# Maxima of the unkept key tiles: score tiles compared with keys on the partitions, in place of products with queries on the partitions

## The chip, the cores and the metric

One core of a Trainium2 chip runs the whole kernel. The metric is the device time of one execution in microseconds; the time shown for a kernel is the median of its runs. One further execution is recorded by the hardware profiler, and the profile's views (busy shares, groups of instructions, timeline, windows, the chain of waits) all tell of that one.

The engines are named as in the profile: PE is TensorE (matrix products; PEld is its weight load), DVE is VectorE, ACT is ScalarE, POOL is GpSimd, and SP issues most of the DMAs. Products go to PSUM[...].

## The reference

Input `x` is (2, 2048, 512) float32, and `cond_1024` is a conditioning vector for each of the two batches. Two blocks follow each other.

1. A conditioned state-space block: a modulated layer norm, a diagonal complex linear recurrence along the 2048 positions (128 states), a gated residual, and then a modulated feed-forward with 2048 hidden features (gelu).
2. A conditioned attention block with 16 heads of 32 features:

```python
h = _sln(hidden, w, ...)                    # layer norm, scaled and shifted by the condition
q, k, v = split(h @ Wqkv.T + bqkv)          # 16 heads of 32
energy = einsum('bhqd,bhkd->bhqk', q, k)
att = softmax(energy, axis=-1) / D ** 0.5
out = einsum('bhqk,bhkd->bhqd', att, v)     # back to (B, N, 512)
out = out @ Wp.T + bp
h1 = out + hidden
return _sln(h1, w, ...) + h1
```

The softmax needs, for each query, the maximum of its scores over all 2048 keys before the exponentials. The change concerns how this maximum is found for a part of the keys.

## The kernel before

**Two parts.** The first part (to about 1400 us) does the state-space block, the feed-forward and the projections to q, k and v, in chunks of 512 positions. Queries, keys and values are written to DRAM, q and k as a high and a low half each (`hi`, `lo`), so that one product with 128 rows of contraction gives the scores of 32 features at close to float32 precision. The second part is the attention, and the change lies in it.

**Blocks and slots.** The attention runs over 64 blocks: a batch, a pair of heads and a chunk of 512 queries. Keys stand in 16 tiles of 128. A score tile `s` is 128 keys on the partitions by 512 queries for each of the two heads, so 128 x 1024 float32, or two PSUM banks. A block is spread over NP = 8 slots (index `i`), and two blocks are under way at a time: in slot `j` the kernel finds maxima for the block that begins 14 slots later (AHEAD), and does exponentials and weighted sums for the block that is current. The code writes the work of each slot in the order in which every engine shall take it (the schedule is manual), and semaphores between engines come from what each instruction reads and writes. A tile of a pool with `bufs=n` takes its turn in a ring of n buffers; a new tile waits until the one that held its buffer before has been read.

**The maxima.** Of the 16 key tiles, NX = 11 are kept: `keep` (L761) makes the score tile on PE (`raw_scores`, L751), ACT copies it to SBUF (L765), and DVE takes the running maximum of the block over it (L770, `runs[n]`). Slots i = 0, 2 and 6 keep two tiles, the others one. The other five tiles (NY) are not kept; their scores are made again later by `make` (L815) in five slots (i = 1, 3, 4, 5, 7), when DVE subtracts the maximum straight from PSUM. For the maxima of these five, `across` (L772) computes in each of the eight slots the scores of 128 queries of one head against all 640 keys, with queries on the partitions (two products of 320 columns into the two banks of tile `m`), and DVE reduces them along the row (L784).

`turn_run` (L786) transposes the running maximum of a block on PE, so that queries stand on the partitions, and DVE reduces over keys (L791); a last reduction (L794) joins this with the results of `across`. These run in slots i = 1 and 2 of the next block, and `spread` (L798) in i = 3: it writes the negated maximum to DRAM and reads it back on all partitions as `shift`.

**The rest of a slot.** `take_off` (L811) adds `shift` to a kept tile on POOL, `exponentials` (L822) runs on ACT, and `weighted` (L827) sums values weighted by the probabilities on PE into `o`, for the two key tiles of the slot before. The order in a slot is: what is due by the table `due`; `make`; `across`; a first exponential; `keep`; a second exponential; work due later in the slot; `take_off`; `weighted`. When a block is finished ACT copies `o` out (L843).

**Output.** Batch 0's output projection, residual and norm run in slots of batch 1's blocks (`project`, `residual`, `statistics`, `gain`), with the projection in the PSUM tag `pt`. For the last batch `project` takes its PSUM tile from the tag `m` (L901), and for the last chunk `end_begin` (L1036) takes one from `m` and one from `s`.

**PSUM in the attention:** `s` two tiles of two banks, `m` two banks, `pt` one and `o` one: eight.

Of the kernel before, what the change touches and what calls it, by code (L numbers as in the profile page):

```python
# [8 lines left out]
F32 = mybir.dt.float32  # L9
# [5 lines left out]
ALU = mybir.AluOpType  # L15
AX = mybir.AxisListType
# [3 lines left out]
P = 128  # L20
# [19 lines left out]
def tile_s5_block_then_sln_attention(  # L40
# [21 lines left out]
    nc = tc.nc  # L62
    NB, L, D = x.shape
    KC = D // P
    CH = 512
    TT = CH // P
# [4 lines left out]
    NKT = L // P  # L71
# [4 lines left out]
    small = ctx.enter_context(tc.tile_pool(name="small", bufs=2))  # L76
# [436 lines left out]
    def at_norm(b, c):  # L513
        normalised(b, c)
        xc = xt.pop((b, c))
        for t in range(TT):
            nc.gpsimd.tensor_tensor(xc[:, t, :], xc[:, t, :], bp_row, ALU.add)
        nc.sync.dma_start(x2[b][c * CH : (c + 1) * CH, :].rearrange("(t p) d -> p t d", p=P), xc)
# [40 lines left out]
    start = order[0]  # L559
# [68 lines left out]
    for i, now in enumerate(order):  # L628
# [36 lines left out]
        def run_due(at):  # L665
            for what, *args in due[at]:
                what(*args)
# [27 lines left out]

    NX = 11
    NY = NKT - NX  # L700
    YW = NY * P // 2
    kpools = [ctx.enter_context(tc.tile_pool(name="kpool0", bufs=2, side="right"))]
    qpool = ctx.enter_context(tc.tile_pool(name="qpool", bufs=4, side="right"))
    ring = ctx.enter_context(tc.tile_pool(name="ring", bufs=22, side="right"))
# [1 line left out]
    ps = ctx.enter_context(tc.tile_pool(name="ps2", bufs=1, space=PSUM, side="right"))  # L706
# [15 lines left out]
    pair_of = [pairs.index((b, p)) for b, p, _ in blocks]  # L722
    kst, qst, shifts, runs, tops = {}, {}, {}, {}, {}
    kept, probs, outs, ends = {}, {}, {}, {"o": [], "by": []}
# [24 lines left out]
            nc.sync.dma_start(vst[i % 2][:, :, 2 * e, :], vd[b][:, f].rearrange("(t p) d -> p t d", p=P))  # L749

    def raw_scores(n, kt):  # L751
        s = ps.tile([P, 2, CH], F32, name="s", bufs=2)
        for e in range(2):
            nc.tensor.matmul(  # L754
                s[:, e, :], kst[pair_of[n], e][:, kt * P : (kt + 1) * P], qst[n][:, e, :],
                start=True, stop=True,
            )
        return s


    def keep(n, kt):  # L761

        s = raw_scores(n, kt)
        x = ring.tile([P, 2, CH], F32, name="x")
        nc.scalar.copy(x, s)  # L765
        kept[n, kt] = x
        if kt == 1:
            runs[n] = rows_r.tile([P, 2, CH], F32, name="run")
        if kt > 0:
            nc.vector.tensor_tensor(runs[n], s, kept[n, 0] if kt == 1 else runs[n], ALU.max)  # L770

    def across(n, e, t):  # L772

        if (e, t) == (0, 0):
            tops[n] = small.tile([P, 2 * TT, 2], F32, name="top", bufs=3)
        m = ps.tile([P, 2, CH], F32, name="m")
        for i in range(2):
            k = NX * P + i * YW
            nc.tensor.matmul(  # L779
                m[:, i, :YW], qst[n][:, e, t * P : (t + 1) * P], kst[pair_of[n], e][:, k : k + YW],  # L780
                start=True, stop=True,
            )
        j = e * TT + t
        nc.vector.tensor_reduce(tops[n][:, j, 0:1], m[:, :, :YW], AX.XY, ALU.max, negate=True)  # L784

    def turn_run(n, e):  # L786

        pt = ps.tile([P, TT, P], F32, name="pt_run", tag="pt")
        for t in range(TT):
            nc.tensor.transpose(pt[:, t, :], runs[n][:, e, t * P : (t + 1) * P], ident)  # L790
        nc.vector.tensor_reduce(tops[n][:, e * TT : (e + 1) * TT, 1], pt, AX.X, ALU.max, negate=True)  # L791
        if e == 1:
            neg = small.tile([P, 2 * TT], F32, name="neg", bufs=3)
            nc.vector.tensor_reduce(neg, tops[n], AX.X, ALU.min)  # L794
            tops[n] = neg
            runs.pop(n)

    def spread(n):  # L798
# [12 lines left out]
    def take_off(n, kt):  # L811
        x = kept[n, kt]
        nc.gpsimd.tensor_tensor(x, x, shifts[n], ALU.add)  # L813

    def make(n, kt):  # L815

        s = raw_scores(n, kt)
        x = ppool.tile([P, 2, CH], F32, name="pT")
        nc.vector.tensor_tensor(x, s, shifts[n], ALU.add)  # L819
        kept[n, kt] = x  # L820

    def exponentials(n, kt):  # L822
        x = kept.pop((n, kt))
        nc.scalar.activation(x, x, AF.Exp)  # L824
        probs[n, kt] = x
# [69 lines left out]
    def project(b, qt, groups=tuple(range(NG))):  # L895

        o4, h, *py = held[b, qt]
        if py:
            py = py[0]
        elif len(groups) == NG:  # L900
            py = ps.tile([P, 2, CH], F32, name="py2", tag="m")[:, 0, :]  # L901
        else:
            py = ps.tile([P, CH], F32, name="py", tag="pt")
        for g in groups:
            nc.tensor.matmul(py, o4[:, g, :], wp[:, g, :], start=g == 0, stop=g == NG - 1)  # L905
        held[b, qt] = o4, h, py
# [128 lines left out]

    def end_begin(i):  # L1036

        if i:
            ends["py", i] = ps.tile([P, 2, CH], F32, name="py4", tag="s", bufs=2)
        else:  # L1040
            ends["py", i] = ps.tile([P, 2, CH], F32, name="py3", tag="m")
        for t in range(2):
            nc.tensor.matmul(ends["py", i][:, t, :], ident, ends["h"][i][:, t, :], start=True, stop=False)

# [9 lines left out]
    def end_last(o):  # L1054
# [4 lines left out]
        for at in parts:  # L1059
            nc.scalar.copy(raw[:, at], o[:, at])  # L1060
        end_begin(1)
        for i, at in enumerate(parts):
            nc.tensor.matmul(turned[:, i, :], ends["turn"], raw[:, at], start=True, stop=True)
# [49 lines left out]
    keeps, m = [], 0  # L1113
# [5 lines left out]
    for i in range(NP):  # L1119
        if (i + AHEAD) % NP in twice:  # L1120
            uses.append([kx, kx + 1])
            kx += 2
        else:
            uses.append([kx, ky])
            kx += 1
            ky += 1
    assert m == NX and kx == NX and ky == NKT

    due = {}
# [21 lines left out]
    for b in range(NB):  # L1151
        for c in range(NQ):
            j = NP * (blocks.index((b, NPAIR - 1, c)) + 1) + 1
            if (b, c) == (LB, LC):
                most, rest = slice(0, NH - 4), slice(NH - 4, NH - 2)
                j = NP * (N - 1)
# [22 lines left out]
            for t in range(TT):  # L1179
                qt = c * TT + t  # L1180
                if b == LB:
                    k = j + 3 + 2 * t
# [8 lines left out]
                else:  # L1191

                    k = NP * (NPAIR * NQ * (b + 1) + 2 + 3 * qt // 2)
# [15 lines left out]
    def block_at(j):  # L1209
        n, i = divmod(j, NP)  # L1210
        return (n, i) if 0 <= n < N else (None, i)

    for j in range(FIRST, NP * N + 2):
        if j == OPEN:
            assert not left
            late.close()
            fixed = ctx.enter_context(tc.tile_pool(name="fixed", bufs=1))
            kpools.append(ctx.enter_context(tc.tile_pool(name="kpool1", bufs=2)))
            ppool = ctx.enter_context(tc.tile_pool(name="ppool", bufs=2))
            rows = ctx.enter_context(tc.tile_pool(name="rows", bufs=2))  # L1220
            work = ctx.enter_context(tc.tile_pool(name="work2", bufs=2))
            ps_o = ctx.enter_context(tc.tile_pool(name="ps_o", bufs=1, space=PSUM))
            vst = [fixed.tile([P, NKT, 3, HD], F32, name=f"v{i}") for i in range(2)]
            for v in vst:
                nc.gpsimd.memset(v[:, :, 1, :], 1.0)
            wp = fixed.tile([P, KC, D], F32, name="wp")
        if j == 2 * NP + 6:
            nc.sync.dma_start(wp, w_pT.rearrange("(k p) f -> p k f", p=P))
        if j == 4 * NP:
            nc.gpsimd.tensor_scalar(wp, wp, ISQ, None, ALU.mult)  # L1230
        run_due(j)
        n, i = block_at(j + AHEAD)
        todo = list(keeps[i]) if n is not None else []
        now, k = block_at(j)
        if now is not None and uses[k][1] >= NX:
            make(now, uses[k][1])
        if n is not None:
            across(n, i // TT, i % TT)
        if now is not None:
            exponentials(now, uses[k][0])  # L1240
        for kt in todo:
            keep(n, kt)
        if j == -AHEAD - 1:
            pieces = TT
        elif -AHEAD <= j < -AHEAD + 2:
            pieces = 2
        elif j >= -AHEAD + 2:
            pieces = -(-len(left) // (OPEN - j)) if j < OPEN else 0
        else:
            pieces = 0  # L1250
        for _ in range(pieces):
            what, *args = left.pop(0)
            what(*args)
        if j == -AHEAD - 1:
            at_norm(*order[-1])
        if now is not None:
            exponentials(now, uses[k][1])
        run_due(j + 0.5)
        n, i = block_at(j + 1)
        if n is not None:  # L1260
            for kt in uses[i]:
                if kt < NX:
                    take_off(n, kt)
        n, i = block_at(j - 1)
        if n is not None:
            for h, kt in enumerate(uses[i]):
                weighted(n, kt, i == 0 and h == 0, i == NP - 1 and h == 1)
# [56 lines left out]
```

## Time and profile before

| | us |
|---|---|
| median of 3 runs (3457.08 to 3461.29) | 3458.43 |
| the profiled execution | 3459.56 |
| its span, first to last instruction | 3457.8 |
| PE busy in the span | 3335.5 (96%) |
| DVE, ACT, POOL busy | 2151.7, 1939.8, 2137.8 |
| DVE maxima over kept tiles, L770 | 640 of 1.22 each |
| DVE reductions of `m`, L784 | 512 of 0.815 each |
| PE products of scores, L754, and of `m`, L779 | 2048 and 1024 |

A row of the timeline gives start, length, engine, line and operation, out<-in with the shape, and how many instructions were merged; in brackets stands the idle time before it and what ended it. PE's products are pipelined and their ends are modelled, so the distance from one start to the next says more than a row's length. A row of the chain of waits gives start, length and work; the chain leads from the last instruction back to what released each step. A window's row gives its length, then the busy time of PE, PE's weight loads, DVE, ACT and POOL with the number of instructions, then TensorE's granted clock, the DMA share and GB/s.

### The profile page before, as it was taken

Reading aid. Unit: us, or ns where it says so; the run is one execution under the profiler, and the core shown is the slowest. Engines: PE = TensorE matmul, PEld = TensorE weight load, DVE = VectorE, ACT = ScalarE, POOL = GpSimd, SP = SyncE. Lnnn points to the kernel's source line nnn. Section 1 sums busy time; section 2 is a strip of 40 time slices with the busy share of each in tenths; the row PEclk is TensorE's granted clock in tenths of the full one; section 3 lists DMA queues with packets and bytes.
Section 4 is the critical chain, followed back from the end, with each engine's and each line's share of the span. In section 5 each row is a group of like instructions: output and inputs, shape, how many; then the busy total and the mean of one; then the engine's idle time right before and its main releaser. Section 6 shows DMA issues by size and latency. Waiting matters only on the chain.

```text
span 3457.8 us, 34348 instructions
## 1 busy us (share of the span) xinstructions
PE 3335.5 (96%) x11764; PEld 1508.3 (44%) x11764; DVE 2151.7 (62%) x2976; ACT 1939.8 (56%) x2208; POOL 2137.8 (62%) x1162
## 2 busy tenths in 40 slices
PE   7999999999999999999999999999999999999997
PEld 4444444444444444444444444444444444444432
DVE  6232323232322310688888888888888888888885
ACT  2111111111111111398999999999888888888963
POOL 4133131313131310289898989998898989899986
PEclk8999999999999999999999999999999999999999
DMA  8001111111110112432223222223234233233233
GB/s 304 1 31 43 43 43 43 43 43 43 43 43 31 43 37 61 121 77 67 58 62 72 66 67 54 72 67 75 70 81 96 65 87 85 71 85 78 61 97 115
DMA packets 201396, 237.06 MB, mean 69 GB/s; under 512 B 89544, under 2 KB 118728, under 8 KB 197126
## 3 DMA queue, kind: packets, MB, share of 16 engines
q1 hardware_dynamic: 201222, 234.87, 24.5%
q8 instruction: 93, 1.52, 0.2%
q14 instruction: 81, 0.66, 0.1%
HBM read 166.77 MB, written 67.76 MB: 68 GB/s over the span
## 4 chain that ended last, share of the span: by engine, by line
PE 73%; DVE 14%; ACT 8%; issue 2%; DMA 1%; POOL 1%; SPq 0%; DVEq 0%; ACTq 0%; POOLq 0%
PE o L834 15%; PE ph L487 13%; PE po L500 13%; PE s L754 10%; DVE run L770 10%; PE pk L530 6%; ACT x L765 4%; PE pv L542 3%; PE m L779 3%; PE py L905 2%; PE pt_run L790 2%; ACT pT L824 2%; ACT x L824 2%; PE pu L421 2%; PE pt_tf L149 1%
## 5 line engine op out<-in xcount | busy, mean ns | idle before, releaser
L813 POOL TENSOR_TENSOR x<-x,shift 128x1024 f32<-128x1024 f32 x704 | 1653.8, 2387 | 153.6 <-DMA shift<-flat 104.6
L765 ACT COPY x<-s 128x1024 f32<-128x1024 f32 x704 | 692.4, 1012 | 213.0 <-PE s L754 211.9
L770 DVE TENSOR_TENSOR run<-s,run 128x1024 f32<-128x1024 f32 x576 | 702.9, 1220 | 73.6 <-ACT x L765 50.2
L824 ACT ACTIVATE x<-x 128x1024 f32<-128x1024 f32 x704 | 739.8, 1060 | 11.9 <-POOL x L813 11.6
L754 PE MATMUL s<-qs,ks 128*128 128x512 f32 x2048 | 669.5, 421 | 51.3 <-DVE run L770 45.2
L834 PE MATMUL o<-x,v 128*64 128x512 f32 x2816 | 718.4, 612 | 0.0
L487 PE MATMUL ph<-fT,w_sb 128*128 128x512 f32 x1024 | 463.5, 597 | 0.0
L500 PE MATMUL po<-w_sb,hid 128*128 128x512 f32 x1024 | 460.3, 592 | 0.0
L754 PEld LDWEIGHTS s<-qs,ks 128*128 128x128 f32 x2048 | 334.4, 189 | 275.4 <-DVE run L770 149.7
L819 DVE TENSOR_TENSOR pT<-s,shift 128x1024 f32<-128x1024 f32 x320 | 389.5, 1217 | 85.1 <-PE s L754 85.1
L784 DVE TENSOR_REDUCE top<-m 128x1 f32<-128x640 f32 x512 | 417.4, 815 | 9.8 <-PE m L779 7.1
L491 ACT ACTIVATE hid<-ph,vec 128x512 f32<-128x512 f32 x128 | 88.0, 687 | 595.9 <-PE ph L487 595.9
L824 ACT ACTIVATE pT<-pT 128x1024 f32<-128x1024 f32 x320 | 339.4, 1061 | 50.2 <-DVE pT L819 50.2
L158 DVE SCALAR_TENSOR_TENSOR lo<-pk,vec,hi 128x512 fp32r<-128x512 f32 x64 | 48.0, 751 | 494.4 <-ACT hi L157 494.4
L834 PE MATMUL o<-pT,v 128*64 128x512 f32 x1280 | 330.5, 595 | 7.9 <-ACT pT L824 7.9
L487 PEld LDWEIGHTS ph<-fT,w_sb 128*128 128x128 f32 x1024 | 193.3, 192 | 228.9 <-issue 228.9
L834 PEld LDWEIGHTS o<-x,v 128*64 128x64 f32 x2816 | 157.1, 135 | 310.4 <-issue 191.4
L434 POOL TENSOR_TENSOR m<-m,m 128x512 f32<-128x512 f32 x8 | 13.1, 1643 | 449.7 <-DVE m L432 449.7
L500 PEld LDWEIGHTS po<-w_sb,hid 128*128 128x128 f32 x1024 | 190.7, 190 | 221.5 <-issue 221.5
L779 PE MATMUL m<-ks,qs 128*128 128x320 f32 x1024 | 256.6, 332 | 17.3 <-DVE top L784 15.5
L157 ACT ACTIVATE hi<-pk,vec 128x512 fp32r<-128x512 f32 x64 | 44.0, 687 | 383.3 <-PE pk L530 383.3
L510 POOL TENSOR_TENSOR x<-x,gated 128x512 f32<-128x512 f32 x32 | 39.6, 1269 | 354.4 <-DVE gated L509 354.4
(253 smaller groups left out, 2774.6 us busy)
## 6 DMA issues: line engine op xcount, KB each, us to landing
ks<-kd SPq DMA_DIRECT2D x128, 256.0 KB
qs<-qd SPq DMA_DIRECT2D x512, 64.0 KB
shift<-flat SPq DMA_DIRECT2D x64, 512.0 KB
x<-in_x SPq DMA_DIRECT2D x8, 1024.0 KB
w_sb<-in_w SPq DMA_DIRECT2D x8, 1024.0 KB
x<-x SPq DMA_DIRECT2D x8, 1024.0 KB
kd<-hi SPq DMA_DIRECT2D x32, 256.0 KB
kd<-lo SPq DMA_DIRECT2D x32, 256.0 KB
```

The lines of the kernel that those rows point to most:

```text
L487: nc.tensor.matmul(ph, w1_sb[:, k, f * P : (f + 1) * P], fts[b, c][:, k, :], start=k == 0, stop=k == KC - 1)
L500: nc.tensor.matmul(pos[b, c][:, t, :], hid[:, t * P : (t + 1) * P], w2_sb[:, f, :], start=f == 0, stop=f == FC - 1,)
L530: nc.tensor.matmul(pk, w[:, k, g * P : (g + 1) * P], hT[:, k, :], start=k == 0, stop=k == KC - 1)
L754: nc.tensor.matmul(s[:, e, :], kst[pair_of[n], e][:, kt * P : (kt + 1) * P], qst[n][:, e, :], start=True, stop=True,)
L765: nc.scalar.copy(x, s)
L770: nc.vector.tensor_tensor(runs[n], s, kept[n, 0] if kt == 1 else runs[n], ALU.max)
L779: nc.tensor.matmul(m[:, i, :YW], qst[n][:, e, t * P : (t + 1) * P], kst[pair_of[n], e][:, k : k + YW], start=True, stop=True,)
L784: nc.vector.tensor_reduce(tops[n][:, j, 0:1], m[:, :, :YW], AX.XY, ALU.max, negate=True)
L813: nc.gpsimd.tensor_tensor(x, x, shifts[n], ALU.add)
L819: nc.vector.tensor_tensor(x, s, shifts[n], ALU.add)
L824: nc.scalar.activation(x, x, AF.Exp)
L834: nc.tensor.matmul(outs[n][64 * e : 64 * e + 64, :], v[:, kt, e : e + 2, :], x[:, e, :], start=first, stop=final,)
```

## The change

`across` and its PSUM tile `m` are gone. In their place `compare` makes one score tile of an unkept key tile, in the same form as `raw_scores` gives for the kept ones (keys on the partitions), and DVE takes it into the running maximum `runs[n]`. It is called at the place of `across`, in the five slots i = 1, 2, 4, 6 and 7, for key tiles 11 to 15. Nothing is copied to SBUF. The two banks that `m` had go to a third score tile: `s` now has three buffers. `turn_run` alone gives the negated maximum, so the reduction that joined two results goes. `project` (last batch) and `end_begin` take their tiles from the tag `s`.

```diff
     def raw_scores(n, kt):
-        s = ps.tile([P, 2, CH], F32, name="s", bufs=2)
+        s = ps.tile([P, 2, CH], F32, name="s", bufs=3)
...
-    def across(n, e, t):
-
-        if (e, t) == (0, 0):
-            tops[n] = small.tile([P, 2 * TT, 2], F32, name="top", bufs=3)
-        m = ps.tile([P, 2, CH], F32, name="m")
-        for i in range(2):
-            k = NX * P + i * YW
-            nc.tensor.matmul(
-                m[:, i, :YW], qst[n][:, e, t * P : (t + 1) * P], kst[pair_of[n], e][:, k : k + YW],
-                start=True, stop=True,
-            )
-        j = e * TT + t
-        nc.vector.tensor_reduce(tops[n][:, j, 0:1], m[:, :, :YW], AX.XY, ALU.max, negate=True)
+    def compare(n, kt):
+
+        nc.vector.tensor_tensor(runs[n], raw_scores(n, kt), runs[n], ALU.max)
 
     def turn_run(n, e):
 
+        if e == 0:
+            tops[n] = small.tile([P, 2 * TT], F32, name="neg", bufs=3)
         pt = ps.tile([P, TT, P], F32, name="pt_run", tag="pt")
         for t in range(TT):
             nc.tensor.transpose(pt[:, t, :], runs[n][:, e, t * P : (t + 1) * P], ident)
-        nc.vector.tensor_reduce(tops[n][:, e * TT : (e + 1) * TT, 1], pt, AX.X, ALU.max, negate=True)
+        nc.vector.tensor_reduce(tops[n][:, e * TT : (e + 1) * TT], pt, AX.X, ALU.max, negate=True)
         if e == 1:
-            neg = small.tile([P, 2 * TT], F32, name="neg", bufs=3)
-            nc.vector.tensor_reduce(neg, tops[n], AX.X, ALU.min)
-            tops[n] = neg
             runs.pop(n)
...
-            py = ps.tile([P, 2, CH], F32, name="py2", tag="m")[:, 0, :]
+            py = ps.tile([P, 2, CH], F32, name="py2", tag="s", bufs=3)[:, 0, :]
...
-        if i:
-            ends["py", i] = ps.tile([P, 2, CH], F32, name="py4", tag="s", bufs=2)
-        else:
-            ends["py", i] = ps.tile([P, 2, CH], F32, name="py3", tag="m")
+        ends["py", i] = ps.tile([P, 2, CH], F32, name="py4", tag="s", bufs=3)
...
+    compares = dict(zip((1, 2, 4, 6, 7), range(NX, NKT)))
...
-        if n is not None:
-            across(n, i // TT, i % TT)
+        if n is not None and i in compares:
+            compare(n, compares[i])
```

More of the change, by code (lines that the diff above doesn't have):

```diff
@@ L699, in tile_s5_block_then_sln_attention @@
     NX = 11
-    NY = NKT - NX
-    YW = NY * P // 2
     kpools = [ctx.enter_context(tc.tile_pool(name="kpool0", bufs=2, side="right"))]
```

## The prediction

> **What bounds the kernel now.** First the busy shares on the page, then one window of the attention part, then the rows of one slot, then the chain of waits. The page and a window of 200 us in the first half of the attention:
>
> ```profile
> PE 3335.5 (96%) x11764; PEld 1508.3 (44%) x11764; DVE 2151.7 (62%) x2976; ACT 1939.8 (56%) x2208; POOL 2137.8 (62%) x1162
> 1800.00:2000.00 200.00, 195.27 (x850) 87.60 (x851) 176.73 (x183) 185.60 (x204) 181.73 (x79) 1.00 0.26 66
> ```
>
> In the window (PE, weight loads, DVE, ACT, POOL) TensorE is busy 97.6%, but ACT 93%, POOL 91% and DVE 88%: nothing has room for much. The copies of `o` (L843) start 28.50 us apart there, block after block, so that is a block's price; in the second half, where the output projection of batch 0 runs beside, three blocks in turn take 33.05, 29.62 and 31.95 (31.5 on average).
>
> TensorE's timeline over two slots, i=6 and i=7 of a block (start, length, operation):
>
> ```profile
> 1816.19 0.56 PE L779 MATMUL m<-ks,qs 128*128 128x320 f32 x2
> 1816.60 1.09 PE L754 MATMUL s<-qs,ks 128*128 128x512 f32 x4
> 1817.61 1.08 PE L834 MATMUL o<-x,v 128*64 128x512 f32 x4
> 1818.52 1.03 PE L834 MATMUL o<-pT,v 128*64 128x512 f32 x4
> 1819.62 0.73 PE L754 MATMUL s<-qs,ks 128*128 128x512 f32 x2
> 1820.18 0.45 PE L779 MATMUL m<-ks,qs 128*128 128x320 f32 x2
> 1820.95 0.73 PE L754 MATMUL s<-qs,ks 128*128 128x512 f32 x2 [0.31 <-DVE run L770]
> 1821.61 1.94 PE L834 MATMUL o<-x,v 128*64 128x512 f32 x8
> 1823.48 0.56 PE L779 MATMUL m<-ks,qs 128*128 128x320 f32 x2
> ```
>
> Start to start, slot i=6 is m 0.41, two score pairs 1.01, eight `o` 1.87: 3.29 us. Slot i=7 takes 3.29 of work too but 4.00 in all: the first pair comes 0.14 late and the second starts 0.77 after m where 0.30 is usual. The chain of waits names the reason:
>
> ```profile
> 1817.41 0.91 ACT x L765
> 1818.32 0.02 issue
> 1818.34 1.24 DVE run L770
> ...
> 1819.67 1.24 DVE run L770
> 1820.90 0.04 issue
> 1820.95 0.73 PE s L754 x2
> ```
>
> Two score buffers, both last read by the running maxima, which come after ACT's copies of the same tiles. Slot i=3, behind the other two-keep slot, loses 0.58 likewise (4.02 against 3.29 and 0.15 for the small transpose). Of 28.50 us some 1.3 is such waiting: the slots' own work (i=0 to 7: 3.28, 3.66, 3.69, 3.44, then 3.29 four times) sums to 27.2.
>
> **What the Trainium skill says.** "TensorE: Matmul & The Clock Gate", Back-to-back issue gap, gives N/2.4 + 2.5 ns: 216 ns for 512 columns, 136 for 320. The trace has 0.225 and 0.15 (a further score pair costs 1.01 - 0.56 = 0.45 us, a pair of m 0.30), near enough; columns count, and 8 x 2 x 320 equals 5 x 2 x 512. "PSUM — Partial Sum Buffer", PSUM bank collisions, says that two engines must not read one bank at once; this agrees with the maximum that starts 0.02 after the copy of its tile ends. "VectorE: DVE Perf Modes", The DRAIN you can't avoid, says that a read of what the instruction before wrote needs a semaphore even on one engine; the trace shows a maximum following a maximum after 1.33 us (1818.34 to 1819.67), an unrelated instruction after 1.13 to 1.15.
>
> **The change part by part**, per block.
> TensorE loses eight pairs of m at 0.29 (2.3 us; where m stood first, the first score pair takes over the 0.1 that follows `o`) and gains five score pairs at 0.45 (2.25). The slots become 3.00 with two pairs, 3.45 with three, 3.84 and 3.85 where the transposes of the running maximum precede (i=1, 2) and 3.15 for i=3: 27.2 us, as before to within 0.1. So the products themselves bring nothing, at most 6 us in 64 blocks.
>
> DVE loses eight reductions (815 ns rows, 0.73 start to start: 5.8) and one small one (0.09 exposed, 1803.47 to 1803.56), and gains five compares. No row is a compare, but the maximum of a kept tile is the same form, 1220 ns; before a dependent maximum it holds the engine for 1.33: 6.65. The block becomes 5 x 1.13 for pT, 5 x 1.33, ten maxima (three before a dependent one) 7 x 1.13 + 3 x 1.33, and 2 x 0.60 for reductions after transposes: 25.4 us, against 25.2 summed the same way from the starts before. It fits in 28.5, but at the block's first maximum DVE also idles (1.66 us in the trace) for ACT's copies.
>
> ACT and POOL issue what they did; no DMA and no queue order changes. The compare sits ahead of the slot's keep on PE and DVE: it puts the keep's scores 0.15 later than m did, hence ACT's copy and the exponential behind it, which ACT's 7% of idle time must cover (if it is gone, 0.15 x 5 slots x 64 = 48 us). The compare tile has one reader, so no ACT copy stands before its release. The last compare of a block ends in i=7, the transposes come in i=1 of the next, 3 us and more later: `shift` is no later, the `neg` reduction even gone.
>
> The third buffer decides. I work the ring by hand: each score tile takes the buffer of the third before it (21 tiles in a block, so it repeats), and waits until DVE has read that, plus 0.05. From i=0 at 0: pairs at 0 and 0.57, end 3.00; DVE's first maximum after the second copy, at 2.95. i=1 from 3.00: the keep wants 4.41, buffer free at 4.22; DVE reduces at 4.08, pT 4.68, compare 5.81, maximum 7.14 to 8.36. i=2 from 6.84: the third pair wants 8.26, free at 8.41: wait 0.15; DVE to 12.75. i=3 from 10.84: none. i=4 from 13.99: 0.06. i=5 from 17.49: none. i=6 from 20.49: none; compare at 21.24, maxima at 22.74 (after the copy) and 24.07 to 25.29. i=7 from 23.93: the keep wants 24.95, free at 25.34: 0.40. End 27.77. Waits 0.6 in place of 1.3; 28.50 becomes 27.77, 0.73 less. The same recurrence with two buffers gives the 0.14 and 0.47 of i=7 seen above, which is why I trust it.
>
> In the second half a query tile adds to PE two groups of 1.72 and to DVE 0.60 (residual), 1.39 (statistics) and 1.26 (gain), in i=5, 6 and 7. Before, the extra over PE's part is (94.62 - 85.5 - 6.88)/2 = 1.1 us per tile; by the same working DVE's lag now costs 0.48 in i=7, 0.66 in i=0 and 0.45 in i=1 and 2, 1.0 more than the plain block. About equal, so 0.73 stays.
> The projections of the last blocks (12 of them) move from m to the score ring. There m lost 0.3 behind each to its residual and 0.5 to the reduction of the slot before; but DVE carries 2.0 us of statistics and as much of Newton steps there, and three-score slots press on it. I put it at nothing, between 4 us gained and 6 lost. The last block holds a buffer from k=6 on with two scores left and two buffers for them: nothing.
>
> Sum: 64 blocks less about 3 for the ramp, where other products fill PE, and the tail: 61 x 0.73 = 45 us. The profiled execution ran 3459.56 us (span 3457.8), 1.1 above the median 3458.43, so I take off the median: 3414 us.
>
> **The rivals.**
> (a) All waits go: DVE's lag absorbed, PE at its 27.2 floor: 61 x 1.3 = 80 us, 3378. For it: PE is the busiest engine; against: DVE's 25.4 plus 2 us of idle at the first maximum leave it 0.4 of slack in 27.8.
> (b) The wait only moves: the keep's scores wait 0.2 to 0.3 in each of the five three-score slots, 1.3 in all again; then within 0.2% (7 us, about what a measurement of this kernel tells from no change). For it: PE's columns are equal and the third pair is in a ring with slower readers.
> (c) Slower: DVE's dependent chain becomes the bound. Place: compare, then maximum, in i=1, 2, 4, 6, 7. If handing over to a dependent maximum costs more, or each waits for the copy behind it, DVE's 25.4 + 2.0 passes 28.5 once the 20 PSUM passes each take 0.06 more. At 0.08 more it is 0.5 us per block, 30 us: 3489. The same sign follows if ACT, delayed by 0.15 in each keep, has no room left. For it: ACT and DVE in the window are at 93% and 88%, and in the second half DVE already stalls PE (m waits 0.68 for a reduction in i=0). Against: rows of the same form are steady (1210 to 1226 ns).
>
> **How the numbers follow.** My forecast, 20 to 62 us gained: 0.52. (a) 0.20. (b), with small gains and losses: 0.12, of which 0.08 within 0.2%. (c) 0.16. Faster by over 0.2%: 0.52 + 0.20 + 0.03 = 0.75; same 0.08; slower 0.17. Likeliest 3414, its own range 3396 to 3438. The 8-in-10 range goes from 3372, just past (a), to 3466, which takes in (b) and the mild end of (c); it leaves out about 0.05 below and 0.12 above.
>
> **What would show it.** Copies of `o` 27.6 to 28.0 us apart in the first half; no rows of m; 960 maxima in place of 640, some 1.22 each; the wait of scores for the running maximum in i=3 gone and in i=7 down to 0.4; DVE over 91% in the window. Wrong if the blocks are 28.5 apart or more: then the waits before the keep's scores, or ACT waiting for scores, have grown, and the rows say which; or if the last three blocks (37.5, 49.1, 38.7 between copies) have lengthened.

## The result and the profile after

The changed kernel takes 3433.77 us (median of four runs, 3429.86 to 3434.69), the kernel before 3459.86 us beside it: ratio 0.9921, 95% interval 0.9906 to 0.9936. That is 26 us less; 45 were forecast. The span of the profiled execution went from 3457.8 to 3431.5 us. First the busy shares on the page of the changed kernel, two of its costliest groups, and the window of 200 us in the first half of the attention:

```profile
PE 3333.8 (97%) x11380; PEld 1450.9 (42%) x11380; DVE 2129.4 (62%) x2720; ACT 1950.2 (57%) x2208; POOL 2140.0 (62%) x1162
...
L767 DVE TENSOR_TENSOR run<-s,run 128x1024 f32<-128x1024 f32 x576 | 705.1, 1224 | 79.4 <-ACT x L762 35.9
...
L771 DVE TENSOR_TENSOR run<-s,run 128x1024 f32<-128x1024 f32 x320 | 389.1, 1216 | 12.5 <-PE s L751 12.1
```

```profile
1800.00:2000.00 200.00, 197.89 (x821) 81.94 (x818) 176.22 (x158) 189.71 (x208) 184.57 (x80) 1.00 0.27 66
```

PE's busy time in the whole span is the same to 2 us: products of equal columns, as worked out. The compares (L771) cost 1216 ns each, like the maxima over kept tiles (L767, 1224 ns). In the window PE rose from 97.6% to 98.9%, ACT from 93% to 95%, and DVE stayed at 88%.

Between the copies of `o` the times are:

| | before | after |
|---|---|---|
| a block in the first half | 28.50 | 28.11 |
| three blocks in the second half | 94.6 | 93.15 |
| the last three | 125.3 | 124.4 |

Added over the 62 distances, the first 32 (the first half) bring 11.9 us, the next 27 bring 13.5 and the last three 0.9. The gain lies in the attention's blocks, as forecast, but is 0.39 us per block there where 0.73 was forecast. TensorE's timeline shows where the rest is. In slot i=3 the second pair of products (a pair makes one score tile) waited before the change:

```profile
1805.74 0.73 PE L754 MATMUL s<-qs,ks 128*128 128x512 f32 x2
...
1807.07 0.74 PE L754 MATMUL s<-qs,ks 128*128 128x512 f32 x2 [0.31 <-DVE run L770]
```

The changed kernel, in slots i=3, then i=6, 7 and the next block's 0, then i=2:

```profile
1801.25 1.24 PE L751 MATMUL s<-qs,ks 128*128 128x512 f32 x4
1802.42 1.94 PE L820 MATMUL o<-x,v 128*64 128x512 f32 x8
...
1810.87 1.67 PE L751 MATMUL s<-qs,ks 128*128 128x512 f32 x6
1812.47 1.08 PE L820 MATMUL o<-x,v 128*64 128x512 f32 x4
...
1814.34 1.20 PE L751 MATMUL s<-qs,ks 128*128 128x512 f32 x4
1815.77 0.73 PE L751 MATMUL s<-qs,ks 128*128 128x512 f32 x2 [0.23 <-DVE run L767]
1816.43 1.94 PE L820 MATMUL o<-x,v 128*64 128x512 f32 x8
1818.30 1.20 PE L751 MATMUL s<-qs,ks 128*128 128x512 f32 x4
1819.43 1.08 PE L820 MATMUL o<-x,v 128*64 128x512 f32 x4
...
1825.57 1.99 PE L751 MATMUL s<-qs,ks 128*128 128x512 f32 x6
1827.49 1.08 PE L820 MATMUL o<-x,v 128*64 128x512 f32 x4
```

From one slot's first start to the next one's, i=3 to i=2 of a block take 3.07, 3.59, 2.99, 3.47, 3.96, 3.00, 3.86 and 4.20 us. Against the work of each slot, 0.51 us is lost in i=7, 0.35 in i=2 and 0.14 in i=4: 1.0 us of waiting, where 1.3 was before and 0.6 was forecast. The wait of i=3 is gone. In i=7 the third pair starts 1.43 us after the start of the first two instead of 1.01, and from it to `o` takes 0.66 us, where an unhindered pair takes 0.56 (in the slot behind, two pairs take 1.13 to `o`). So a wait costs its own length and 0.10 for the restart. The weight loads of the same two stretches:

```profile
1814.34 0.76 PEld L751 LDWEIGHTS s<-qs,ks 128*128 128x128 f32 x4 [0.81 <-issue]
1815.77 0.30 PEld L751 LDWEIGHTS s<-qs,ks 128*128 128x128 f32 x2 [0.67 <-DVE run L767]
```

Behind the wait the load of the weights begins together with its product, at 1815.77. One by one, the second product of that pair starts 0.34 us after the first, as it does where scores follow `o` (1814.34); inside a stream the products start 0.23 apart. The waits of i=2 and i=4 end the same way. The chain of waits of the changed kernel at the same place:

```profile
1812.12 1.02 ACT x L762
...
1813.16 1.24 DVE run L767
...
1814.49 1.24 DVE run L767
...
1815.77 0.73 PE s L751 x2
```

It is the chain of before: scores, ACT's copy, a maximum, a second maximum that depends on it, and only then the buffer for PE.

### The profile page after: what moved, and what is told of

Read it like the earlier page. It is cut to its first block, busy times and chain, and to the rows that moved or that the text cites. A ratio compares the mean times of both kernels' runs of the same rounds, so it can differ in the third digit from the quotient of the medians.

```text
span 3431.5 us, 33641 instructions
## 1 busy us (share of the span) xinstructions
PE 3333.8 (97%) x11380; PEld 1450.9 (42%) x11380; DVE 2129.4 (62%) x2720; ACT 1950.2 (57%) x2208; POOL 2140.0 (62%) x1162
## 4 chain that ended last, share of the span: by engine, by line
PE 61%; DVE 16%; ACT 16%; issue 3%; DMA 2%; POOL 2%; SPq 0%; DVEq 0%; ACTq 0%; POOLq 0%
PE ph L487 13%; PE po L500 13%; PE o L820 9%; DVE run L767 8%; PE s L751 7%; ACT x L762 7%; PE pk L530 6%; ACT x L810 4%; ACT pT L810 4%; PE pv L542 3%; DVE pT L805 3%; PE py L891 2%; DVE run L771 2%; PE pu L421 2%; POOL x L799 1%
## 5 line engine op out<-in xcount | busy, mean ns | idle before, releaser
L751 PE MATMUL s<-qs,ks 128*128 128x512 f32 x2688 | 823.2, 427 | 41.3 <-DVE run L767 28.4
L767 DVE TENSOR_TENSOR run<-s,run 128x1024 f32<-128x1024 f32 x576 | 705.1, 1224 | 79.4 <-ACT x L762 35.9
L751 PEld LDWEIGHTS s<-qs,ks 128*128 128x128 f32 x2688 | 444.2, 189 | 455.1 <-DVE run L767 159.2
L771 DVE TENSOR_TENSOR run<-s,run 128x1024 f32<-128x1024 f32 x320 | 389.1, 1216 | 12.5 <-PE s L751 12.1
L820 PEld LDWEIGHTS o<-pT,v 128*64 128x64 f32 x1280 | 91.4, 137 | 193.8 <-issue 142.2
```

The source lines that it names most:

```text
L751: nc.tensor.matmul(s[:, e, :], kst[pair_of[n], e][:, kt * P : (kt + 1) * P], qst[n][:, e, :], start=True, stop=True,)
L771: nc.vector.tensor_tensor(runs[n], raw_scores(n, kt), runs[n], ALU.max)
L820: nc.tensor.matmul(outs[n][64 * e : 64 * e + 64, :], v[:, kt, e : e + 2, :], x[:, e, :], start=first, stop=final,)
```

## The experiments

My theory was that the gain is the shared third buffer acting with the new compare tiles, and that what is left are waits for a score buffer behind DVE's maxima. The first rival: one half of the change alone pays. The second: ACT, at 95%, is the new bound. The two runs that split the change and the four that leave a part out are one execution each; executions of the same kernel differ here by up to 0.4%, so the distances between copies of `o`, nearly the same block after block, are the safer figures.

**Compares with a PSUM tile of their own.** The scores of kept and remade tiles have a ring of two, as before the change, and the last projections go back to the tile `m`.

```diff
-    def raw_scores(n, kt):
-        s = ps.tile([P, 2, CH], F32, name="s", bufs=3)
+    def raw_scores(n, kt, tag="s", bufs=2):
+        s = ps.tile([P, 2, CH], F32, name="s", tag=tag, bufs=bufs)
...
-        nc.vector.tensor_tensor(runs[n], raw_scores(n, kt), runs[n], ALU.max)
+        nc.vector.tensor_tensor(runs[n], raw_scores(n, kt, "m", 1), runs[n], ALU.max)
...
```

> The compare tile has a PSUM tile of its own (two banks, one buffer) and the other scores a ring of two, as before the change; the last projections are back in that tile. My theory, that the shared third buffer is what pays: the waits of slots i=3 and i=7 come back behind maxima that now start later, about 2.4 us of waiting per block, so the copies of o stand 29.0 to 29.5 us apart in the first half and the time is 3480 to 3510 us. Rival, that the new form of the products pays by itself and the ring is only along: 28.1 to 28.3 us per block, 3430 to 3445 us.

Measured: 3551.12 us, 29.99 us per block. Worse than the forecast's range by some 40 us, and on the side of the theory. TensorE's timeline of this run in slot i=3:

```profile
1820.35 0.27 PE L787 MATMUL pt_neg<-ident,neg 128*8 128x128 f32 x1
1820.73 0.73 PE L751 MATMUL s<-qs,ks 128*128 128x512 f32 x2
1822.06 0.72 PE L751 MATMUL s<-qs,ks 128*128 128x512 f32 x2 [0.60 <-DVE run L767]
```

The second pair comes 1.33 us after the first where 0.57 is its work, and the first already waits 0.35. The loss is 1.1 us in i=3, 0.6 each in i=5 and i=0, and 0.4 in i=7; only i=3 and i=7 were expected. The new form of the products, with the buffers as they were, costs 91 us.

**`across` in a ring of three.** The kernel before, its tile `m` taking turns with the scores.

```diff
-        s = ps.tile([P, 2, CH], F32, name="s", bufs=2)
+        s = ps.tile([P, 2, CH], F32, name="s", bufs=3)
-        m = ps.tile([P, 2, CH], F32, name="m")
+        m = ps.tile([P, 2, CH], F32, name="m", tag="s", bufs=3)
...
```

The last projections take their tiles from the same ring.

> The kernel before with its tile m in one ring of three with the scores. By hand every slot then has three tiles, each waits for the tile at its own place in the slot before, and the last one of i=3 and i=7 still waits for the second maximum of the slot before. My theory (buffers pay only together with slots that have two tiles): 28.3 to 28.6 us per block, 3445 to 3465 us. Rival, that the third buffer alone pays: 28.1 us or less, 3435 us or less.

Measured: 3459.72 us, 28.5 us per block: nothing, as forecast. So neither half pays by itself. Form alone: 91 us slower; ring alone: no difference; both: 26 us faster.

**DVE lighter.** Each compare takes only the first head's half.

```diff
-        nc.vector.tensor_tensor(runs[n], raw_scores(n, kt), runs[n], ALU.max)
+        s = raw_scores(n, kt)
+        nc.vector.tensor_tensor(runs[n][:, 0, :], s[:, 0, :], runs[n][:, 0, :], ALU.max)
```

> The changed kernel, but DVE takes only the first head's half of each compare tile into the running maximum (so the second head's maximum leaves out five key tiles); PE's products stay. DVE has 5 x 0.53 us less per block. My theory: the waits of i=2 (0.35) and i=4 (0.14) go, that of i=7 stays because the maximum there waits for ACT's copy; 27.6 to 27.8 us per block, 3400 to 3415 us. Rival, ACT is the bound: 28.0 to 28.2 us, 3428 to 3438 us.

Measured: 3407.82 us, 27.66 us per block. In the timeline of TensorE the slot i=7 keeps its wait, while i=2 (pairs 1817.57, `o` 1819.15) has none any more:

```profile
1807.76 0.73 PE L751 MATMUL s<-qs,ks 128*128 128x512 f32 x2 [0.23 <-DVE run L767]
...
1817.57 1.65 PE L751 MATMUL s<-qs,ks 128*128 128x512 f32 x6
1819.15 1.08 PE L821 MATMUL o<-x,v 128*64 128x512 f32 x4
```

Both as the theory had it. Of the 0.14 in i=4, which was to go too, 0.09 stays.

**ACT lighter.** The exponentials of the unkept tiles for the first head only.

```diff
-        nc.scalar.activation(x, x, AF.Exp)
+        y = x if kt < NX else x[:, 0, :]
+        nc.scalar.activation(y, y, AF.Exp)
```

> The changed kernel, but the exponentials of the five unkept tiles are taken for the first head only (the second head's stay as they are, so its sums leave out those exponentials). ACT has 5 x 0.43 us less per block, nothing else changes. Theory, PE waits for buffers behind DVE: at most 0.2 us comes off, 27.9 to 28.1 us per block, 3420 to 3434 us. Rival, ACT at 95 percent is the bound: 27.2 to 27.6 us per block, 3380 to 3405 us.

Measured: 3419.50 us, 27.85 us per block, just below the theory's band and above the rival's. Taking 2.1 us of ACT off a block yields 0.27. ACT is not the bound, but it is in the chain: the block's first maximum, which waits for ACT's copy, starts 0.21 us before i=1 instead of 0.06 after it, and slot i=2 falls from 4.20 us to 3.93; i=7 stays at 3.96.

**Both lighter.** The two edits together.

> The changed kernel with both reliefs: DVE compares the first head only, and the exponentials of the five unkept tiles are taken for the first head only (those parts of the second head's maximum and sums are left out). Alone the first took 0.45 us off a block and the second 0.27. If DVE's maxima and ACT's copies make one chain before PE, the two together come near TensorE's own 27.1 us: 27.2 to 27.5 us per block, 3375 to 3395 us. Rival, something else holds PE (the weights' reload, or POOL): no better than the first alone, 27.66 us and 3405 us.

Measured: 3391.55 us, inside the theory's band. But in the first half it is 27.65 us per block, no better than DVE's relief alone, which is what the rival had: there the block is TensorE's own 27.1 and the 0.5 of slot i=7, where the third pair still waits:

```profile
1803.19 0.72 PE L751 MATMUL s<-qs,ks 128*128 128x512 f32 x2 [0.23 <-DVE run L767]
```

In the second half three blocks take 91.7 us, against 92.5 and 92.7 with one relief. So in the first half the two reliefs remove the same wait, that of i=2, and i=7 is out of reach for either. What holds PE there is the theory's chain and not the rival's "something else": the next run shows it.

**Without the last link of i=7's chain.** No maximum over the second tile kept in i=6.

```diff
-        if kt > 0:
+        if kt > 0 and kt != 9:
```

> The changed kernel without DVE's maximum over the second tile kept in i=6 (key tile 9 is left out of the maximum; its copy, exponential and products stay). Theory: the wait of i=7 is a chain of latencies (scores, ACT's copy, one maximum, the next maximum, then the buffer); without its last link the buffer is free after the copy, and the whole 0.5 us goes: 27.5 to 27.7 us per block, 3396 to 3410 us. Rival, DVE's load alone counts: half of the compares (2.65 us of DVE) gave 0.45, so 1.24 us gives 0.2: 27.9 us per block, 3420 us.

Measured: 3403.78 us, inside the theory's band, but 27.85 us per block in the first half, as the rival had it. TensorE's timeline, i=7, then i=1 to the start of i=2:

```profile
1807.53 1.67 PE L751 MATMUL s<-qs,ks 128*128 128x512 f32 x6
1809.13 1.94 PE L820 MATMUL o<-x,v 128*64 128x512 f32 x8
...
1813.99 0.66 PE L779 MATMUL pt_run<-ident,run 128*128 128x128 f32 x4
1814.41 1.89 PE L751 MATMUL s<-qs,ks 128*128 128x512 f32 x6
...
1818.09 0.66 PE L779 MATMUL pt_run<-ident,run 128*128 128x128 f32 x4
```

The wait in i=7 is gone (three pairs in 1.60). Half of every compare, 2.65 us of DVE's work in a block, had left it standing, so the chain was its cause and not DVE's load. But i=1 now takes 4.10 us where it took 3.86. PE comes to i=1 half a microsecond sooner, and meets there the buffer that the block's first maximum holds; this starts only after ACT's copies of i=0, at 1814.28, 0.28 us into i=1. In the second half three blocks fall from 93.15 to 90.6; ACT is less busy there (88% in 2560 to 2760 us of the changed kernel, against 95%), which may be why, but no run tests it.

**Compares in other slots.** Six runs move them; nothing is left out of the computation.

```diff
-    compares = dict(zip((1, 2, 4, 6, 7), range(NX, NKT)))
+    compares = dict(zip((1, 3, 4, 5, 7), range(NX, NKT)))
```

> The changed kernel with its five compares in slots i=1, 3, 4, 5, 7, none in a slot that keeps two tiles. My theory, that what is left are score tiles waiting for a buffer behind DVE's maxima: DVE's work per slot is more even (no slot has three dependent maxima), the wait of i=7 (0.5 us) goes, that of i=2 goes, and 0.4 and 0.2 appear in i=3 and i=4; 27.6 to 27.8 us per block, 3400 to 3415 us. Rival, that ACT (95 percent busy) is the new bound: it does the same work, 28.0 to 28.2 us per block, 3428 to 3438 us.

Measured: 3457.79 us (ratio to before 0.999, 0.9981 to 0.9998), 28.73 us per block. Both expectations missed. The timelines of ACT, DVE and PE in this run, put in order of time:

```profile
1812.30 1.01 ACT L762 COPY x<-s 128x1024 f32<-128x1024 f32 x1 [0.68 <-PE s L751]
...
1815.12 1.92 ACT L762 COPY x<-s 128x1024 f32<-128x1024 f32 x2
1816.15 2.55 DVE L767 TENSOR_TENSOR run<-s,run 128x1024 f32<-128x1024 f32 x2 [1.14 <-ACT x L762]
...
1818.76 0.73 PE L751 MATMUL s<-qs,ks 128*128 128x512 f32 x2 [0.55 <-DVE run L767]
```

The compare stands ahead of the keep's scores, so in three slots running ACT waits 0.5 to 0.7 us for them. It arrives late at the two copies of i=6, DVE idles 1.14 us until the first of them is done, and PE's third pair in i=7 starts 0.7 late. My working had given DVE its even load and forgotten ACT.

```diff
-    compares = dict(zip((1, 2, 4, 6, 7), range(NX, NKT)))
+    compares = dict(zip((1, 2, 4, 5, 6), range(NX, NKT)))
```

> The changed kernel with its last compare moved from slot i=7 to i=5, so that the slot behind the two keeps of i=6 has only two score tiles. Theory now: the tile that waits in i=7 is the third one, whose buffer the second keep of i=6 had, released by the chain copy, maximum, maximum; with two tiles in i=7 that wait (0.5 us) goes, and 0.1 to 0.3 appear in i=5 and i=6, where DVE lags: 27.8 to 28.0 us per block, 3412 to 3427 us. Rival, ACT behind the later scores of i=5, as in the run with compares in 1, 3, 4, 5, 7: 28.4 us or more, 3450 us or more.

Measured: 3462.19 us (1.001, 1.0001 to 1.0018), 28.45 us per block: a miss, and the rival's numbers. The wait of i=7 did go (2.99 us), and a larger one, 0.6, came two slots on, in i=1. In time order, from the timelines of ACT, DVE and PE:

```profile
1808.02 1.01 ACT L762 COPY x<-s 128x1024 f32<-128x1024 f32 x1 [0.69 <-PE s L751]
...
1819.94 1.23 DVE L767 TENSOR_TENSOR run<-s,x 128x1024 f32<-128x1024 f32 x1 [2.50 <-ACT x L762]
...
1821.22 0.73 PE L751 MATMUL s<-qs,ks 128*128 128x512 f32 x2 [0.32 <-DVE run L767]
```

ACT loses 0.69 in i=5, right before its two heavy slots and the copy of `o`, and has no idle time above 0.02 us from there to the block's first maximum; that maximum is late, and the third pair of i=1 waits.

The other four use slot i=0, between its two keeps; the compare then starts the running maximum from its own scores and the first kept tile:

```diff
-    compares = dict(zip((1, 2, 4, 6, 7), range(NX, NKT)))
+    compares = dict(zip((0, 1, 4, 5, 6), range(NX, NKT)))
...
         for kt in todo:
             keep(n, kt)
+            if kt == 0:
+                compare(n, compares[0])
...
```

> As the run before, and the compare of i=2 goes to i=0, between the two keeps (it starts the running maximum from its own scores and the first kept tile). It fills the 2 us in which DVE idles there and leaves i=2, where two reductions' worth of DVE work stood, with two tiles. Theory: the waits of i=2 (0.35) and i=4 (0.14) go too; 27.2 to 27.5 us per block, 3380 to 3398 us. Rival, ACT bound or DVE still late: 27.8 us or more, 3412 us or more.

Measured: 3441.10 us (0.995, 0.9935 to 0.9965). 27.94 us per block in the first half, better than the changed kernel's 28.11, but short of the forecast and on the rival's side; three blocks of the second half take 95.1, worse than its 93.15. The next run gives the blocks that carry batch 0's projection another set.

> The run with compares in 0, 1, 4, 5, 6, but the blocks whose slots also carry batch 0's projection (n = 36 to 59) take their compares in i=0 to 4. Theory: in those blocks DVE's residual, statistics and gain stand in i=5, 6 and 7, so compares there make DVE late; in i=3 and 4 PE has 1.7 us of projection more and DVE room. First half 27.9 us per block as before, three blocks of the second half 91 to 92.5 us (93.1 in the changed kernel, 95.1 in the run before); 3405 to 3430 us. Rival, ACT is what holds the second half: no change there, 3438 us or more.

```diff
-    compares = dict(zip((0, 1, 4, 5, 6), range(NX, NKT)))
+    early_set, late_set = (0, 1, 4, 5, 6), (0, 1, 2, 3, 4)   # late_set for 36 <= n < 60
...
```

Measured: 3457.43 us (0.9992, 0.9983 to 1.0001): three blocks of the second half take 97.1 us, a miss in the wrong direction. TensorE's timeline of this run in i=0 of such a block:

```profile
2662.07 0.73 PE L751 MATMUL s<-qs,ks 128*128 128x512 f32 x2 [0.18 <-DVE pT L806]
2663.20 0.74 PE L751 MATMUL s<-qs,ks 128*128 128x512 f32 x2 [0.40 <-DVE run L765]
```

DVE's statistics (2659.40 to 2660.87) make it late with `pT` and the maximum of i=7, and the second and third tile of i=0 wait for these two. That is one slot of one block; how the whole loss of the second half divides was not taken apart.

> As the run before, with the other blocks' compares in 0, 1, 4, 6, 7 (the changed kernel's, but i=0 for i=2). Theory: the wait of i=2 goes, that of i=7 (0.5) stays, and ACT does not wait for a late keep in i=5; 27.5 to 27.8 us per block in the first half, 3398 to 3420 us. Rival: ACT, waiting for the keep's scores in i=1 and i=7, holds it at 27.9 or more, 3425 us or more.

```diff
-    early_set, late_set = (0, 1, 4, 5, 6), (0, 1, 2, 3, 4)
+    early_set, late_set = (0, 1, 4, 6, 7), (0, 1, 2, 3, 4)
```

Measured: 3449.47 us (0.9972, 0.9963 to 0.9981), with the same loss in the second half, so the total misses the forecast, and 27.77 us per block in the first, inside the band: the changed kernel's compare of i=2 is better placed in i=0. That made the last version.

> Compares in 0, 1, 4, 6, 7 (27.77 us per block measured in the first half) for the blocks without batch 0's projection, and in the changed kernel's 1, 2, 4, 6, 7 for those with it (93.1 us for three blocks measured). 34 blocks x 0.34 less than the changed kernel: 3420 to 3425 us, ratio to the kernel before 0.988 to 0.990. If the two sets disturb each other at their border, or the last blocks lose, 3428 us or more.

```diff
-    early_set, late_set = (0, 1, 4, 6, 7), (0, 1, 2, 3, 4)
+    early_set, late_set = (0, 1, 4, 6, 7), (1, 2, 4, 6, 7)
...
```

Measured: 3420.48 us (ratio to before 0.9879, 0.9862 to 0.9897), with 27.78 us per block in the first half and 93.2 for three in the second. It is as forecast, and faster than both kernels.

## Why the prediction was right or wrong

The direction and the range held; the size did not: 26 us of the 45.

TensorE's part, "the products themselves bring nothing", is right: 3333.8 us busy against 3335.5, and slots of 3.0 and 3.45 us as worked out. The DVE rows are right (1216 ns), and nothing on POOL or the DMAs moved. The block's idle time at its first maximum was put at some 2 us; it is 2.05. The sign "DVE over 91% in the window" failed, with 88% before and after. The 25.4 us are right if the gaps of 0.10 us before a block's six dependent maxima are counted in; the profile counts them as idle, and by its busy time, which is what the 25.2 of before was, a block takes DVE 24.75 us now.

The step that was mis-sized is the ring: "Waits 0.6 in place of 1.3; 28.50 becomes 27.77". Its places are right (i=2, i=4, i=7, and none in i=3), its sizes were 0.15, 0.06 and 0.40, and the trace has 0.35, 0.14 and 0.51: 0.39 more in all. (The slots' own work is 0.05 less than forecast, so the block misses by 0.34.) Some 0.3 of the 0.39 is one term: each of the three waits ends with a restart of 0.10 us on PE, which I had counted in the 1.3 of before, since that came from slot lengths, and left out of the 0.6, which came from buffer times alone. Two sums of different kinds were compared. The other 0.1 is the first maximum, at 0.06 us after i=1 begins instead of 0.05 before it; the third pair of i=2 waits that much longer. The remark that the same recurrence "gives the 0.14 and 0.47 of i=7 seen above, which is why I trust it" should have warned me: those make 0.61, and the slot had lost 0.71.

"About equal, so 0.73 stays" for the second half: measured 0.50 per block (94.6 to 93.15 for three), so the second half gains somewhat more than the first, not the same. What in it differs by 0.1 was not taken apart. The last blocks, put "at nothing", gave 0.9 us (38.3, 47.3 and 38.7 us between copies: the first a little longer, the second shorter).

Rival (a), all waits gone, was not near: even with both reliefs a block stays at 27.65. Rival (b), the wait only moves, is what happened to a part of it: the 0.58 of i=3 went and the 0.71 of i=7 became 0.51, but 0.35 in i=2 and 0.14 in i=4 are new. Rival (c), DVE's dependent chain as the bound, did not come. With a tile of their own for the compares the waits behind dependent maxima cost 91 us, but DVE is busy only 83% of the window there (166.4 of 200 us), so that is the length of a chain and not DVE's load. And the sentence that the 0.15 by which the keep's scores come later must be covered by ACT's idle time named what the theory for the compares in 1, 3, 4, 5, 7 then forgot.

## What to carry to other kernels

When a ring of buffers ties engines together, price a wait with the restart behind it, and take both sides of a comparison from the same kind of measure (slot lengths against slot lengths). A saved wait need not add up: the engine that no longer waits arrives sooner at the next buffer. Of the 0.5 us saved in i=7, half came back in i=1 when a maximum was left out, and more than all of it when a compare was moved to i=5. Where work may be placed in several slots, ask for each place which in-order queue it delays (here the kept tile's copy on ACT), not only which engine has room; seven placements of the same five compares gave 3420 to 3462 us.

## What was not expected of the hardware

The restart of 0.10 us after a wait on PE (0.66 from the score pair to `o` instead of 0.56) was new to me, and it is in every run: behind a wait the second product of a pair starts 0.34 us after the first, inside a stream 0.23. The weights' load, which there begins together with its product instead of ahead of it, would fit; no run took it away, so the cause is not shown. On DVE nothing more was found than the two distances of the forecast: in every run an fp32 maximum over a score tile in PSUM is followed after 1.13 to 1.14 us by an unrelated instruction and after 1.31 to 1.33 by one that reads its result.
